# Gate and up of the second layer as one product of 26 block products, with weight sums made in the first layer

## The chip, the cores and the metric

The kernel runs on one core of a Trainium2 chip. The metric is the device time of one execution in microseconds. Three runs of the kernel before took 867.36, 867.67 and 868.07 us; the median is 867.67. The engines are called by these names: TensorE (PE in the profile, PEld for its weight loads), VectorE (DVE), ScalarE (ACT), GpSimd (POOL) and SyncE (SP, which issues the DMAs).

## The reference

Two feed-forward layers follow each other on x of 4 x 512 tokens and 512 features, in float32, each with a residual sum and layer norms without weights:

```
x = x + layernorm(layer1(layernorm(x)))
x = x + layernorm(layer2(layernorm(x)))

layer1(x): s = silu(x @ Wg.T)              # 2048 x 1376
           s = s with the half of each row that is smallest in |s| set to 0
           return (s * (x @ Wu.T)) @ Wd.T
layer2(x): return (silu(x @ Vg.T) * (x @ Vu.T)) @ Vd.T
```

All six weights have 1376 x 512 elements. They come to the kernel transposed, with the contracted dimension first.

## The kernel before

**First layer.** 2048 tokens are 16 tiles of 128, taken two at a time as eight units (`Unit`). For a unit, `products` makes the gate plainly (L433, four contraction chunks, columns in three pieces) and the up product by a seven-product scheme (class `Seven`, L133: 2x2 by 2x2 blocks from 7 block products in place of 8, with sums of the operands made ahead and sums of the products made behind). `search` finds the row threshold by six counts on ScalarE (L485) with small VectorE steps between. `turns` transposes the product, and `finish` makes the down product, again by seven products (`downs`, L234), whose weights are read piece by piece from DRAM (`down_right`, L220, three buffers). These stages of different units overlap: during the gate of unit j the lists `gate` and `up` in `layers` place the down product of unit j-3, the transposes of unit j-2 and the search of unit j-1.

Sums of weights that the seven-product schemes need are made once on VectorE, in `presum` (L180): it loads four blocks of 128 x 1280, makes four sums and stores them to DRAM. Key "a" (down of layer 1) is made in unit 0; "f" (down of layer 2), "g" and "u" (gate and up of layer 2) in unit 1.

**Second layer.** The tokens are four blocks of 512 (`Block`). `norm` normalises and transposes four tiles into xT. `sums` makes four sums of xT on VectorE (`moving_sums`, L125; tile T). Then five groups follow. Group a stands for two pieces of 128 rows of the gate and the two of the same numbers of the up (rows a*128 and 640 + a*128). `pair` (L682) makes both with `Seven`: 7 products each, with two contraction halves in each, so 28 products of 128 x 128 by 256 columns. A product keeps its bank until VectorE has added it to the output (L154 to L168). The product of `silu(gate)` and up is made by L698 and L702, and `down_sums` (L721) makes sums of it on GpSimd (L119 to L122). The last 96 rows of gate and up go through `rest` (L704), one more `Seven`. `finish` (L737) makes the down product and `out_norm` (L344) normalises it, adds the residual and stores.

PSUM has eight banks here: tags pa, px and py with two each for products, and pt with two for transposes.

**What sets the order.** Each engine works off its own instructions in a fixed order. A scheduler at build time chooses that order from a model of the times, with the program's order as priority. `tc.issue_after(i)` puts what is issued inside it behind instruction i on its engine. After the groups of a block the norms of the next block are issued behind `block.mark` (the group's last multiplication), then the next block's `sums`, then this block's `finish`. In block 0 the `finish` of the last unit of layer 1 stands between `sums` and the first group.

The code ends with a second, general path for rows with ties, under a test at run time; it is not taken in these runs.

Of the kernel before, what the change touches and what calls it, by code (L numbers as in the profile page):

```python
# [29 lines left out]

@with_exitstack
def sandwich_kernel(
# [10 lines left out]
):  # L43

# [20 lines left out]
    HC = FULL // 2  # L65
    HF = HC * P
# [26 lines left out]
    presums = {k: dram.tile([4, P, HC * H2], F32, name=f"sum_{k}") for k in ("a", "f", "g", "u")}  # L93
# [86 lines left out]
    def presum(work, key, w_d):  # L180


        down = key in "af"
        bufs = dict(wd=3, hT=2)

        def load(r, c, tag, k):
            t = work.tile([P, HC * H2], F32, tag=tag, name=f"ps_{key}_{k}", bufs=bufs[tag])
            if down:
                src = w_d[r * HF : (r + 1) * HF, c * H2 : (c + 1) * H2]
            else:  # L190
                src = w_d[c * 2 * P : (c + 1) * 2 * P, r * HF : (r + 1) * HF]
            n = HC if down else 2
            nc.sync.dma_start(
                t.rearrange("p (k h) -> p k h", k=n), src.rearrange("(k p) h -> p k h", p=P)
            )
            return t

        def keep(k, t):
            nc.sync.dma_start(presums[key][k - 1], t)

        x = load(0, 1, "wd", "x") if down else load(1, 0, "wd", "x")
        y = load(0, 0, "wd", "y") if down else load(1, 1, "wd", "y")
        z = load(1, 1, "hT", "z") if down else load(0, 0, "hT", "z")
        w = load(1, 0, "wd", "w") if down else load(0, 1, "wd", "w")
        if down:
            nc.vector.tensor_sub(y, x, y)
        else:
            nc.vector.tensor_add(y, x, y)
        keep(1, y)
        nc.vector.tensor_sub(x, z, x)  # L210
        keep(3, x)
        if down:
            nc.vector.tensor_sub(z, z, y)
        else:
            nc.vector.tensor_sub(z, y, z)
        keep(2, z)
        nc.vector.tensor_sub(w, w, z)
        keep(4, w)

# [157 lines left out]
    class Unit:  # L377
# [205 lines left out]
        def turns(self, other=False):  # L583
# [4 lines left out]
            def turn(k, g0):  # L588
                nm = f"{self.nm}_{self.tiles[k]}"
                if g0 == 0:  # L590
                    if other:
                        if k == 0:
                            self.ends = self.work.tile(
                                [P, 2, P], F32, tag="S", name=f"he{nm}", bufs=1
                            )
                        t = self.big.tile([P, 2 * HC, P], F32, tag="b5", name=f"hT{nm}")
                        end = self.ends[:, k, :]
                    else:
                        t = self.work.tile([P, NI, P], F32, tag="hT", name=f"hT{nm}")
                        end = t[:, NI - 1, :]  # L600
                    self.hT.append((t, end[: isz[-1], :]))
                h, (hT, end) = self.p[k], self.hT[k]
                n = min(4, NI - g0)
                pt = psum.tile([P, 4, P], F32, tag="pt", name=f"ph{nm}_{g0}")
                for c in range(n):
                    i = g0 + c
                    nc.tensor.transpose(
                        pt[: isz[i], c, :], h[:, i * P : i * P + isz[i]], ident
                    )
                nf = n if g0 + n <= FULL else n - 1  # L610
                copy = nc.vector.tensor_copy if other and k else nc.scalar.copy
                copy(hT[:, g0 : g0 + nf, :], pt[:, :nf, :])
                if nf < n:
                    copy(end, pt[: isz[-1], nf, :])
# [39 lines left out]
    class Block:  # L654
# [15 lines left out]
        def sums(self):  # L670
            t = [
                self.big.tile([P, 2, 2, N2], F32, tag="b5", name=f"T{self.nm}_{self.b}_{q}")
                for q in range(2)
            ]
            self.right = moving_sums(
                nc.vector,
                *[half[:, :, cols] for half in self.xT for cols in (slice(N2), slice(N2, N))],
                t[0][:, 0], t[0][:, 1], t[1][:, 0], t[1][:, 1],
            )
            self.h = []  # L680

        def pair(self, a, lefts):  # L682
# [6 lines left out]
            sg = self.work.tile([P, 4, N2], F32, tag="w", name=f"sg{nm}", bufs=1)  # L689
            ms = []  # L690
            for k, left, c in zip("gu", lefts, (sg, h)):
                left = {p: w[:, :, ts(a, P)] for p, w in left.items()}
                m = Seven(f"{k}b{nm}", left, self.right, c[:, 1, :], c[:, 2, :], c[:, 3, :])
                m.first()
                ms.append(m)
            c11g, c11u = [m.second() for m in ms]
            nc.scalar.activation(sg[:, 0, :], c11g, AF.Silu)  # L697
            nc.vector.tensor_mul(h[:, 0, :], sg[:, 0, :], c11u)  # L698
            ms[0].third()
            nc.scalar.activation(sg[:, 1:, :], sg[:, 1:, :], AF.Silu)  # L700
            ms[1].third()
            self.mark = nc.vector.tensor_mul(h[:, 1:, :], sg[:, 1:, :], h[:, 1:, :]).ins  # L702

        def rest(self, left):  # L704

            n = I - 2 * HF
            nm = f"{self.nm}_{self.b}"
            t = self.work.tile([P, 4, N2], F32, tag="w", name=f"sgr{nm}", bufs=1)[:n]
            m = Seven(f"rb{nm}", left, self.right, t[:, 0, :], t[:, 1, :], t[:, 2, :])
            m.first()  # L710
            c11 = m.second()
            h = self.big.tile([P, N], F32, tag="b5", name=f"hTb{nm}_r")
            lo, hi = h[:n, :N2], h[:n, N2:]
            nc.scalar.activation(lo, c11, AF.Silu)
            m.third()
            nc.scalar.activation(hi, m.c12, AF.Silu)
            nc.vector.tensor_mul(lo, lo, m.c21)
            nc.vector.tensor_mul(hi, hi, m.c22)
            self.h.append(h)
# [17 lines left out]
        def finish(self, which, wr, final=False):  # L737

            pairs = []
            for q in which:  # L740
                last = lambda i, q=q: self.h[-1][: isz[-1], ts(q + 2 * i, P)]
# [23 lines left out]
    def layers(nm, general):  # L765
        with ExitStack() as sctx:
# [4 lines left out]
            def extra(k, layer):  # L771
                return [
                    wpool.tile([P, 2, 2 * Q], F32, tag=f"w{k}s{q}", name=f"w{k}s{q}{layer}{nm}")
                    for q in range(3)
                ]

# [23 lines left out]
            t1, t2, t4 = extra("u", 1)  # L800
# [23 lines left out]
            else:  # L824
                wr = last_rows(a_wd, 1)
                w_ds = dict(a=a_wd, f=f_wd, g=f_wg, u=f_wu)
                sums_at = {0: "a", 1: "fgu"}
                for j in range(NU):
# [22 lines left out]
                    for k in sums_at.get(j, ""):  # L851
                        presum(work, k, w_ds[k])
                steps = finish(units[-3:-1], wr)
# [14 lines left out]
            lefts, ws = [], []  # L868
            for k, w_d in (("g", f_wg), ("u", f_wu)):
                w = wpool.tile([P, NH, I], F32, tag="w" + k, name=f"w{k}2{nm}")  # L870
                s1, s2, s4 = [y[:, :, :HF] for y in extra(k, 2)]
                a11, a12, a21, a22 = [
                    w[:, 2 * c : 2 * c + 2, r * HF : (r + 1) * HF] for r in range(2) for c in range(2)
                ]
                for q, a in ((1, s1), (2, s2), (3, a21), (4, s4)):
                    nc.sync.dma_start(a, presums[k][q - 1].rearrange("p (k h) -> p k h", k=2))
                for a, c, r in ((a11, 0, 0), (a12, 1, 0), (a22, 1, 1)):
                    nc.sync.dma_start(
                        a,
                        w_d[c * 2 * P : (c + 1) * 2 * P, r * HF : (r + 1) * HF].rearrange(  # L880
                            "(k p) h -> p k h", p=P
                        ),
                    )
                nc.sync.dma_start(
                    w[:, :, 2 * HF :], w_d[:, 2 * HF :].rearrange("(k p) h -> p k h", p=P)
                )
                lefts.append(dict(p1=a11, p2=a12, p3=s4, p4=a22, p5=s1, p6=s2, p7=a21))
                ws.append(w)
            blocks[0].sums()
            if not general:  # L890
                for f in units[-1].turns():
                    f()
                units[-1].down_sums()
                for f in finish([units[-1]], wr):
                    f()
            wr = last_rows(f_wd, 2)
            t = work.tile([P, 3, 2, I - 2 * HF], F32, tag="S", name=f"wrs{nm}", bufs=1)
            rest = stationary_sums(
                nc.vector,
                *[w[:, 2 * c : 2 * c + 2, 2 * HF :] for w in ws for c in range(2)],  # L900
                t[:, 0], t[:, 1], t[:, 2],
            )
            for b, block in enumerate(blocks):
                last = b + 1 == len(blocks)
                for a in range(HC):
                    block.pair(a, lefts)
# [3 lines left out]
                block.rest(rest)  # L910
# [53 lines left out]
```

## Time and profile before

| | |
|---|---|
| median of three runs | 867.67 us |
| the profiled execution | 867.17 us |
| its span, first to last instruction | 865.4 us |
| TensorE busy | 854.2 us, 3642 matmul records |
| VectorE busy | 533.7 us |
| ScalarE busy | 302.5 us |
| GpSimd busy | 98.8 us |
| DMA | 112.96 MB moved |
| first layer | to about 430 us |
| blocks of the second layer start at | 553.2 (1), 655.2 (2), 757.6 us (3) |

The profile is of one execution. In a group's row stand the line, the engine, the operation, out<-in tiles with shapes, the count, then busy us and mean ns of one, then the engine's idle time before and what ended it. A row of a timeline has start, length, engine, line, operation and tiles. Matmuls are pipelined, so the mean of one is its passage and not the spacing of a stream. Matmuls in float32 leave two records each.

### The profile page before, as it was taken

What the parts mean: (1) busy time and instruction counts of PE and PEld (TensorE: products, weight loads), DVE (VectorE), ACT (ScalarE), POOL (GpSimd) and SP (SyncE); (2) the same over time, 40 slices, a digit from 0 to 9 for tenths busy, and PEclk for the clock granted to TensorE, in tenths of its full rate; (3) what the DMA queues carried; (4) which work ended last, traced back from release to release, by engine and by line L of the source; (5) the groups of instructions that cost most, each with busy time, mean ns of one, the idle gap of its engine ahead of it and who ended that gap; (6) DMA issues with size and microseconds to landing.
All of it is one profiled execution on the core that took longest, in us unless ns stands there. A gap on an engine that the chain in (4) does not pass through costs nothing.

```text
span 865.4 us, 10342 instructions
## 1 busy us (share of the span) xinstructions
PE 854.2 (99%) x3642; PEld 659.6 (76%) x3642; DVE 533.7 (62%) x1432; ACT 302.5 (35%) x601; POOL 98.8 (11%) x178
## 2 busy tenths in 40 slices
PE   9999999999999999999999999999999999999996
PEld 5556566767667676677888888888888888888885
DVE  5887787776949677667955445544436445454434
ACT  3465575647474755656111111011111112011100
POOL 1000000000000001000001220121301222012111
PEclk9999999999999999999999999999999999999999
DMA  9999414334233333387573005500054001430032
GB/s 334 372 329 347 177 55 123 122 100 163 67 116 108 123 122 104 100 323 262 169 242 119 0 1 170 189 2 0 18 183 159 1 0 46 153 125 1 0 100 100
DMA packets 60381, 112.96 MB, mean 131 GB/s; under 512 B 4705, under 2 KB 34529, under 8 KB 60321
## 3 DMA queue, kind: packets, MB, share of 16 engines
q1 hardware_dynamic: 60176, 111.95, 38.4%
q8 instruction: 31, 0.51, 0.2%
q14 instruction: 30, 0.24, 0.1%
q10 hardware_dynamic: 144, 0.26, 0.1%
HBM read 93.32 MB, written 18.87 MB: 130 GB/s over the span
## 4 chain that ended last, share of the span: by engine, by line
PE 51%; DVE 2%; ACT 1%; DMA 1%; issue 0%; POOL 0%; ACTq 0%; DVEq 0%
PE pxub L144 6%; PE pxgb L144 6%; PE pxdb L260 6%; PE paub L144 4%; PE pagb L144 4%; PE pydb L260 4%; PE pyub L144 4%; PE pygb L144 4%; PE padb L260 3%; PE pxd L260 2%; PE pyd L260 2%; PE pxrb L144 1%; PE pad L260 1%; ACT ja L485 1%; PE parb L144 1%; PE ptb L373 1%
## 5 line engine op out<-in xcount | busy, mean ns | idle before, releaser
L485 ACT ACTIVATE ja<-v,cur 128x1376 bf16<-128x1376 f32 x96 | 138.4, 1441 | 64.1 <-DVE cur L510 43.0
L433 PE MATMUL pg<-wg,xT 128*128 128x456 f32 (+1 forms) x384 | 154.8, 549 | 0.2 <-ACT p L437 0.2
L433 PEld LDWEIGHTS pg<-wg,xT 128*128 128x128 f32 x384 | 71.9, 190 | 62.7 <-issue 57.6
L144 PE MATMUL pau<-wu,xT 128*128 128x344 f32 x128 | 43.1, 453 | 0.0
L144 PE MATMUL paub<-xTb,wu 128*128 128x256 f32 x160 | 41.3, 380 | 0.1
L144 PE MATMUL pagb<-xTb,wg 128*128 128x256 f32 x160 | 41.1, 379 | 0.0
L144 PE MATMUL pxub<-T,wu 128*128 128x256 f32 x160 | 41.1, 379 | 0.0
L144 PE MATMUL pxgb<-T,wg 128*128 128x256 f32 x160 | 41.1, 379 | 0.0
L260 PE MATMUL pad<-wd_p,hT 128*128 128x256 f32 x160 | 38.9, 380 | 0.1
L437 ACT ACTIVATE p<-pg 128x456 f32<-128x456 f32 (+1 forms) x48 | 26.0, 543 | 36.4 <-PE pg L433 33.1
L260 PE MATMUL pydb<-wdb_p,D 128*128 128x256 f32 x160 | 37.3, 379 | 0.0
L490 DVE TENSOR_SCALAR low<-cur 128x2 int32<-128x2 f32 x48 | 7.9, 165 | 47.1 <-ACT ja L485 46.7
L260 PE MATMUL pxd<-wd_p,hT 128*128 128x256 f32 x160 | 36.8, 379 | 0.0
L119 POOL TENSOR_TENSOR D<-hTb 128x256 f32<-128x256 f32 x20 | 14.6, 729 | 193.9 <-DVE hTb L702 193.9
L260 PE MATMUL padb<-wdb_p,hTb 128*128 128x256 f32 x160 | 36.7, 379 | 0.0
L260 PE MATMUL pxdb<-wdb_p,hTb 128*128 128x256 f32 x160 | 36.2, 379 | 0.0
L260 PEld LDWEIGHTS pad<-wd_p,hT 128*128 128x128 f32 x160 | 29.9, 190 | 6.7 <-DMA wd_p<-in_L_attn_w_down_dram 0.5
L260 PEld LDWEIGHTS pxd<-wd_p,hT 128*128 128x128 f32 x160 | 30.4, 190 | 5.5 <-issue 0.4
L700 ACT ACTIVATE sg<-sg 128x768 f32<-128x768 f32 x20 | 16.9, 843 | 50.3 <-DVE sg L168 50.3
L110 POOL TENSOR_TENSOR rs_o<-ve_o,nhalf 128x1 f32<-128x1 f32 x16 | 11.5, 731 | 198.0 <-DVE ve_o L108 198.0
L144 PEld LDWEIGHTS paub<-xTb,wu 128*128 128x128 f32 x160 | 30.3, 190 | 4.5 <-ACT sg L697 0.4
L260 PEld LDWEIGHTS pxdb<-wdb_p,hTb 128*128 128x128 f32 x160 | 30.4, 190 | 4.2
(245 smaller groups left out, 1699.5 us busy)
## 6 DMA issues: line engine op xcount, KB each, us to landing
wd_p<-sum_a SPq DMA_DIRECT2D x28, 640.0 KB, 4.0
wd_p<-in_L_attn_w_down_dram SPq DMA_DIRECT2D x21, 640.0 KB, 3.9
wdb_p<-sum_f SPq DMA_DIRECT2D x16, 640.0 KB, 4.0
wdb_p<-in_L_ffn_W_down_dram SPq DMA_DIRECT2D x12, 640.0 KB, 3.9
xn<-in_x_dram SPq DMA_DIRECT2D x16, 256.0 KB, 4.1
xr<-in_x_dram SPq DMA_DIRECT2D x16, 256.0 KB, 4.1
x<-y SPq DMA_DIRECT2D x16, 256.0 KB, 3.1
xnb<-x SPq DMA_DIRECT2D x16, 256.0 KB, 4.1
```

What stands on the lines that cost most here:

```text
L110: nc.gpsimd.tensor_tensor(rs, ve, nhalf, ALU.pow)
L119: eng.tensor_add(s1, a21, a22)
L144: nc.tensor.matmul(ps, self.left[k][:, c, :], self.right[k][:, c, :], start=first and c == 0, stop=c == 1, skip_group_check=not first,)
L260: nc.tensor.matmul(p[which], p[1](k, c), ws[k][:, c, :], start=first and c == 0, stop=c == HC - 1, skip_group_check=not first,)
L373: nc.tensor.transpose(pt[:, c, :], xn[:, ts(c, P)], ident)
L433: nc.tensor.matmul(pg, self.xT[:, i, c, :], wg[:, c, c0:c1], start=(c == 0), stop=(c == NH - 1),)
L437: nc.scalar.activation(p[:, c0:c1], pg, AF.Silu)
L485: nc.scalar.activation(junk, v, AF.Sign, bias=cur[:, 0, i : i + 1], accum_out=cur[:, 1, i : i + 1],)
L490: nc.vector.tensor_scalar(low, cur[:, 1, :], 0.0, None, ALU.is_gt)
L700: nc.scalar.activation(sg[:, 1:, :], sg[:, 1:, :], AF.Silu)
```

## The change

**One product for gate and up.** `group` takes the place of `pair`. Tokens (two halves of 256) by contraction (four chunks of 128) is a 2x4 matrix of blocks, contraction by output rows (two of gate, two of up) a 4x4 one. Their product, 32 block products done plainly and 28 before, is made from 26. A line of `PRODUCTS` is one matmul: the bank it goes to (0 to 5), the operand from xT or its sums, the weight operand, and which outputs get the bank's content added or subtracted after it (outputs 0 to 3 for the first half of the tokens, 4 to 7 for the second; by remainder of 4: gate, gate, up, up). Products go on accumulating in a bank, so after an addition the next product into the same bank waits until it has been read, and a bank is read several times.

```diff
+PRODUCTS = (
+    (0, 10, 17, "+2"), (1, 13, 23, "+6"), (2, 14, 24, "+1"), (0, 25, 21, "+6"), (1, 24, 8, "+2"),
+    (3, 3, 12, "+1"), (0, 11, 22, "+4"), (2, 23, 11, "-4-7"), (1, 8, 0, "+0"), (4, 7, 7, "+7"),
+    (3, 20, 13, "+3"), (5, 16, 3, "-7"), (1, 12, 6, "+4"), (0, 15, 2, "+0"), (4, 21, 5, "+5"),
+    (3, 1, 1, "+0"), (1, 4, 9, "+5"), (5, 22, 4, "+0+1"), (0, 2, 25, "+3"), (2, 19, 16, ""),
+    (1, 17, 20, "+1"), (4, 5, 15, "+4"), (0, 9, 14, "+7"), (2, 7, 19, "-6"), (5, 18, 10, ""),
+    (5, 3, 18, "+2"),
+)
```

(In the file each product has a line of its own.)

```diff
-        def pair(self, a, lefts):
+        def group(self, a, w):
...
+            kw = dict(tag="w", bufs=1) if a % 2 == 0 else dict(tag="c")
+            sg = self.work.tile([P, 4, N2], F32, name=f"sg{nm}", **kw)
+            banks, begun = {}, set()
+            left = {m: sum(o % 4 == m for p in PRODUCTS for o in form(p[3])) for m in range(4)}
+            for k, xv, wv, adds in PRODUCTS:
+                first = k not in banks
+                if first:
+                    tag = ("pa", "px", "py")[len(banks) % 3]
+                    banks[k] = bank(tag, f"{tag}b{nm}_{k}")[:, :N2]
+                with ExitStack() as order:
+                    if self.product is not None:
+                        order.enter_context(tc.issue_after(self.product))
+                    self.product = nc.tensor.matmul(
+                        banks[k], w[wv], self.left[xv], start=first, stop=True,
+                        skip_group_check=not first,
+                    ).ins
+                fresh = False
+                for o, s in form(adds).items():
+                    q, m = divmod(o, 4)
+                    c = (sg, h)[m // 2][:, m % 2 * 2 + q, :]
+                    if o in begun:
+                        add = nc.vector.tensor_add if s > 0 else nc.vector.tensor_sub
+                        self.mark = add(c, c, banks[k]).ins
+                    elif fresh:
+                        nc.vector.tensor_scalar(c, banks[k], float(s), None, ALU.mult)
+                    else:
+                        nc.scalar.mul(c, banks[k], float(s))
+                        fresh = True
+                    begun.add(o)
+                    left[m] -= 1
+                    f = m % 2
+                    part = slice(2 * f, 2 * f + 2)
+                    if m == f and not left[f]:
+                        nc.scalar.activation(sg[:, part], sg[:, part], AF.Silu)
+                    if not left[f] and not left[2 + f]:
+                        nc.vector.tensor_mul(h[:, part], sg[:, part], h[:, part])
```

An output's first value is written by ScalarE, later ones are added by VectorE; the mark is the last such add.

**Sums of the tokens.** `Block.sums` makes 18 sums of 128 x 256 on VectorE (`LEFT_SUMS`) in place of four of 128 x 512. In block 0 they are issued behind the last unit's `down_sums`.

**Sums of the weights.** `presum` keeps "a" and "f". For gate and up `weight_sums` is called at the end of units 0 to 4, for groups 4 down to 0: four loads of 256 KB into a tile `area` of 26 operands (16 blocks of weights, ten places more), 17 sums in place (`RIGHT_SUMS`, 15 of two operands at once and two of one), and, except for group 0, a store of the tile to DRAM.

```diff
+        def after_last(part):
+            last = next(
+                i for i in reversed(nc.cur_bb.bb.instructions)
+                if i.engine == mybir.EngineType.DVE
+            )
+            with tc.issue_after(last):
+                for t in part:
+                    step(t)
+        n = 4
+        parts = [RIGHT_SUMS[q : q + n] for q in range(0, len(RIGHT_SUMS), n)]
...
-                sums_at = {0: "a", 1: "fgu"}
+                sums_at = {0: "a", 1: "f"}
+                area = wpool.tile([P, NP, P], F32, tag="ws", name="area")
...
+                    g = NG + 0 - 1 - j
+                    if 0 <= g < NG:
+                        for f in weight_sums(area, g):
+                            f()
```

Group 0 stays in `area`; the 104 operands of groups 1 to 4 are loaded into the tiles that held the first layer's weights.

**The last 96 rows.** `rest` makes gate and up plainly, four contraction chunks of 512 columns each, with SiLU on ScalarE and one multiplication on VectorE; the four weight sums for it go. In block 0 it stands ahead of the last unit's down product.

```diff
-            blocks[0].sums()
-            if not general:
+            if general:
+                blocks[0].sums()
+            else:
                 for f in units[-1].turns():
                     f()
                 units[-1].down_sums()
+                last = nc.cur_bb.bb.instructions[-1]
+                assert last.engine == mybir.EngineType.DVE
+                with tc.issue_after(last):
+                    blocks[0].sums()
+                blocks[0].rest(w_rest)
                 for f in finish([units[-1]], wr):
                     f()
```

Smaller moves: the ends of the hidden tiles of the last units but one get a tag of their own ("he"), and the scratch of a group alternates between the tags "w" and "c".

## The prediction

> **What bounds the kernel now.** I read the page's head first, then the stretches of time, the groups by shape, the chain of waits and the timeline at a change of block.
>
> ```profile
> PE 854.2 (99%) x3642; PEld 659.6 (76%) x3642; DVE 533.7 (62%) x1432; ACT 302.5 (35%) x601; POOL 98.8 (11%) x178
> ```
>
> TensorE is busy for 99% of the span. That matmuls overlap could hide gaps, so the spacing decides, not this share. The chain of waits names few others and gives the spacing:
>
> ```profile
> PE 51%; DVE 2%; ACT 1%; DMA 1%; issue 0%; POOL 0%; ACTq 0%; DVEq 0%
> ```
>
> ```profile
> 639.84 4.32 PE padb L260 x20
> 644.16 0.86 PE padb L266 x4
> ```
>
> 20 records take 4.32 us: 0.216 us each. In fp32 every product of 128x128 by 256 columns leaves two records (the second layer's groups show 20 x 28 x 2 = 1120), so a product costs 0.432 us. Stretches of the first and second layer (PE, PEld, DVE, ACT, POOL, clock, DMA):
>
> ```profile
> 50.00:100.00 50.00, 50.00 (x148) 27.52 (x147) 43.52 (x106) 24.99 (x52) 1.42 (x4) 1.00 0.83 304
> 200.00:250.00 50.00, 50.00 (x193) 33.48 (x192) 37.51 (x118) 30.57 (x57) 2.68 (x6) 1.00 0.39 124
> 655.00:757.00 102.00, 102.00 (x482) 88.66 (x481) 50.83 (x120) 14.98 (x35) 18.89 (x28) 1.00 0.21 68
> ```
>
> TensorE has no gap in any of them, at full clock. VectorE works 75% of a first-layer stretch and half of a block. So a product taken away is worth its 0.432 us, as long as VectorE follows.
>
> The Trainium skill, "Perfetto Trace Analysis", section "Identifying the Most-Contended Engine", says matmul busy time misjudges headroom and weight loads should be read: by that, 88.66 of 102 leaves 13% free on TensorE and the saving could vanish into slack. The spacing above says otherwise: 0.19 us of load in every 0.216 us slot is 88% with no slot empty. The measurement decides; by the rule the sum would be near zero.
>
> **TensorE, the certain part.** A group of one block drops from 28 products (7 of two contraction halves, gate and up) to 26. 20 groups x 2 x 0.432 = 17.3 us saved. The 96 left-over rows go from 14 products, 6.05 us, to 8 plain ones of 512 columns. The nearest wide row is 16 records of 456 columns in 6.28 us; less the last one's overhang of 0.165 that is 0.382 each, the same 0.84 ns a column as 256 columns show. So 512 columns give 0.43 a record, 0.86 a product, 6.9 a block: 4 x 0.83 = 3.4 us lost. Net -13.9 us.
>
> **VectorE in a group, and the waits of the banks.**
>
> ```profile
> L154 DVE TENSOR_TENSOR sg<-sg,pxgb 128x256 f32<-128x256 f32 x20 | 8.4, 420 | 7.0 <-ACT sg L153 6.6 <-PE pxgb L144 0.4
> L153 ACT COPY sg<-pagb 128x256 f32<-128x256 f32 x20 | 7.4, 372 | 67.5 <-PE pagb L144 34.5 <-DVE hTb L702 32.9
> L127 DVE TENSOR_TENSOR T<-xTb 128x512 f32<-128x512 f32 x4 | 2.8, 688 | 2.9 <-ACT xTb L375 2.9
> ```
>
> The table of products asks for 26 updates of outputs: 8 first ones, which go to ScalarE at 0.37, and 18 adds on VectorE at 0.42, beside two multiplications of 512 elements at 0.69. VectorE gets 18 x 0.42 + 2 x 0.69 = 8.9 us in 26 x 0.432 = 11.2, against 11 x 0.42 + 0.96 = 5.6 in 12.1 now. It fits, but it is no longer slack. ScalarE has 8 x 0.37 + 2 x 0.6 = 4.2 (its rows show 0.54 for 456 and 0.84 for 768 elements).
>
> Now a bank is written again before the group ends, so products wait for reads. In the timeline at 553.17 two products run, their end is due at 554.03 and the copy starts at 554.23: 0.20 after the last slot. A product begun at t is thus read from t+0.63 and free at t+1.00 (ScalarE) or t+1.05 (VectorE). At 437.48 a ScalarE read ends and the weight load that waited starts at 437.53: 0.05. The load runs 0.216 ahead of its product. A bank is reused three products later at the soonest, load at t+1.08, against 1.05 and 1.10: one reuse by VectorE per group is 0.02 late. VectorE's queue (two adds for one product, then the next) makes another up to 0.1 late. 20 groups x 0.02 to 0.12 = 0.4 to 2.4 us; I take 1.
>
> **Starts of blocks.** Here in-order VectorE is still at the normalisation of the block before:
>
> ```profile
> 655.00 0.85 DVE L329 TENSOR_TENSOR yb<-yb,pydb 128x256 f32<-128x256 f32 x2 [0.53 <-PE pydb L266]
> 655.76 1.28 DVE L104 BATCH_NORM_STATS2 st_ob<-yb 128x6 f32<-128x512 f32 x2
> 656.96 0.30 DVE L106 BATCH_NORM_AGGREGATE mv_ob<-st_ob 128x2 f32<-128x6 f32 x2
> 657.22 0.42 DVE L154 TENSOR_TENSOR sg<-sg,pxgb 128x256 f32<-128x256 f32 x1
> ...
> 658.63 1.42 DVE L359 SCALAR_TENSOR_TENSOR yb<-yb,rs_ob,xrb 128x512 f32<-128x512 f32 x2
> 659.96 0.41 DVE L154 TENSOR_TENSOR hTb<-hTb,pxub 128x256 f32<-128x256 f32 x1
> ```
>
> The block starts at 655.23, VectorE is free at 660. One add slipped in at 657.22, the other stood behind both L359 and cost nothing, since its bank was not needed. In the new order the add of product 4 (numbered from 0) is ready at 655.23 + 4 x 0.432 + 0.63 = 657.59 and its bank is due for product 8 at 658.69. Placed where the second L154 stands it ends at 660.38; product 8 starts at 660.64, 1.95 late. Slipped in at 658.5 it costs 0.5, then product 10 another 0.6. If product 3's add stands behind L359 too, product 6, due at 657.82, is 2.8 late; if the order puts adds first, nothing is lost. So 0 to 2.8 a block, and 1.5 from the trace's own mix; three blocks: 4.5 (0 to 8.4).
>
> The sums over the tokens grow from 4 x 0.69 to 18 x 0.42 = 7.6 us on VectorE. Before blocks 1 to 3 they lie beside 34 us of down products, where VectorE has more than half free: nothing. Before block 0 they are pinned after the last unit's transposed sums, which end at 440.25, so they end near 448. Today seven products of group 0 at 0.86, 6.05 us, fill the holes of 433.86 to 450.93; afterwards the 6.9 us of left-over rows must. Its weights land last of the loads. I take +1 (-1 to 4).
>
> **First layer.** Gone: 8 subtractions at 1.49 and 4 at 0.35, 13.3 us. New: per unit 0 to 4, 15 sums of 256 elements at 0.42 and 2 of 128 at about 0.3 (the 192-element row shows 0.35): 6.9, in all 34.5. A 50 us stretch leaves VectorE 12.5 idle, and the second unit carried 12 x 1.49 = 17.9 of such sums (50 to 100 in the view above) with TensorE full. That cover hides it; without it a search chain would be up to 6.9 a unit later, against one unit of slack. On SyncE's queue: 8 loads and 8 stores of 640 KB leave, 20 loads of 256 KB and 4 stores of 1664 KB come, now also in units 2 to 4, where the 640 KB loads of down weights land in 4 us and are wanted soon after. A store in front could delay one by up to 4 us in three units: 0 to 12, nearest to the loads that already share the queue at no price. I take 1. The second layer's loads shrink from 14 x 640 KB to 104 x 64 KB, at the same place.
>
> **Sum.** -13.9 + 1 + 4.5 + 1 + 1 = -6.4. The profiled execution took 867.17 (span 865.4 and 1.8 around it), which gives 860.8; the median shown lies 0.5 above it, so 861.3.
>
> The skill's "VectorE: DVE Perf Modes", section "Rules for kernel authors", speaks against the change: keep the number of operations on VectorE small, since each waits for the pipeline to empty. By its reading every add would stand alone, which the 0.42 us above already charges; it changes the sum only where adds queue.
>
> **Rivals.** First, a clean cover: adds come first in VectorE's order, stores disturb nothing. -13.9 + 0.5 gives 853.8 profiled, 854.3. For it: 8.9 of 11.2 us fits. Against it: the trace's L359 ahead of the add. Chance 0.25.
>
> Second, VectorE's backlog drags: 2.8 at each of four block starts, 2.4 in groups and no net cover in the first layer, about 12 lost: 866 to 869, no measurable change. For it: VectorE goes from 46% to 80% inside groups and cannot catch up in one. Chance 0.12.
>
> Third, slower: the hand-over of a bank takes longer than I read. It sits at three reuses per group at distance three. The group saves 0.86 and the left-over rows take back 0.17, so it decides when each of the three is 0.23 us late, a hand-over of 1.3 instead of 1.05. At 1.45, 20 x 3 x 0.37 = 22 us are lost and with the 4.5 of block starts it ends near 882 (-13.9 + 22 + 4.5 + 2). Against it: the 0.05 us release at 437.53. Chance 0.15.
>
> That the change does not do what it says would mean TensorE's records do not fall by 80 in the groups; the tables leave no room for that.
>
> **How the numbers follow.** Forecast (faster, 856 to 865.9) 0.48, clean 0.25, backlog 0.12, slow hand-over 0.15. A run of this kernel tells about 0.2%, 1.7 us, from no change. Faster 0.73, same 0.12, slower 0.15. The range takes in clean and backlog with the bounds of 0.4 in groups: 853.5 to 869.5.
>
> **What would show it.** Group products: 1040 records at 0.216, left-over rows 64 at 0.43. Right: a block's period falls from 102.3 to near 100.6 (5 x 0.864 less 0.83 saved, 1.5 and 0.25 waited), and weight loads wait for VectorE's adds for some 1.5 us at each block's start and hardly inside groups. Wrong: TensorE idle in the first layer after a late down weight; waits spread over all groups; a hole above 2 us between 430 and 460.

## The result, and the profile after

The changed kernel takes **859.30 us** (median of five runs, 858.18 to 860.42), the kernel before 867.36 in the five runs beside them. The ratio is 0.9908, 95% interval 0.9894 to 0.9923: 8.1 us faster. The profiled execution took 859.3 with a span of 857.4, against 865.4 before: 8.0 less.

The head of the page after:

```profile
PE 842.7 (98%) x3514; PEld 635.5 (74%) x3514; DVE 615.2 (72%) x1697; ACT 345.5 (40%) x713; POOL 100.7 (12%) x178
```

TensorE has 128 records fewer: 80 in the groups and 48 in the left-over rows (14 products of two records became eight, per block). VectorE has 81 us more work, and TensorE's share falls from 99 to 98%: the holes have grown. The chain of waits can't show them, because it breaks off at the last instructions:

```profile
DVE 0%; issue 0%; POOLq 0%
```

So the timeline has to be read. Stretches of time (length, then busy us of PE, PEld, DVE, ACT, POOL, clock, DMA share, GB/s):

```profile
50.00:100.00 50.00, 50.00 (x149) 27.70 (x148) 41.55 (x124) 30.40 (x56) 1.76 (x4) 1.00 0.55 198
200.00:250.00 50.00, 50.00 (x195) 33.93 (x194) 41.77 (x130) 29.72 (x56) 3.83 (x4) 1.00 0.45 138
430.00:462.00 32.00, 30.43 (x130) 21.56 (x128) 20.27 (x50) 6.15 (x16) 1.82 (x3) 1.00 0.67 222
553.00:655.00 102.00, 101.33 (x460) 84.14 (x458) 68.58 (x177) 26.33 (x66) 19.70 (x30) 1.00 0.26 84
```

The first layer is as full as it was. In the changeover (430 to 462) 1.57 us of TensorE are free by this view, against 0.51 before. In a block of the second layer VectorE goes from half to two thirds and TensorE loses 0.67. The rows of the new work:

```profile
L824 DVE TENSOR_TENSOR sg<-sg,pxb 128x256 f32<-128x256 f32 x80 | 33.7, 421 | 18.9 <-PE pxb L814 16.5 <-PE pyb L814 0.4
L828 ACT ACTIVATE hTb<-pab 128x256 f32<-128x256 f32 x40 | 15.4, 384 | 57.6 <-PE pab L814 52.4 <-PE pxd L374 5.2
L846 PE MATMUL parb<-xTb,w_rest 128*96 128x512 f32 x32 | 14.6, 594 | 0.0
```

VectorE's adds take 421 ns each and ScalarE's first writes 384, and over the run both wait mostly for TensorE; TensorE waits for them only in the places listed below.

**Where the time went.** I counted TensorE's late time: from each start, subtract the starts before it plus their records at their spacing (0.216 us for 256 columns, 0.43 for 512). The 17.3 less 3.4 of the prediction's certain part is 13.9; what came back is this:

| place | us late beyond before |
|---|---|
| first layer (last transposes ahead of the changeover at 429.40, before 429.92) | -0.5 |
| changeover, 430 to 460 (2.95, before 1.33) | +1.6 |
| first group of block 0 | +0.4 |
| a down weight of block 0 lands late, 536.26 (1.3, before 0.3) | +1.0 |
| starts of blocks 1, 2, 3 | +1.2, +0.6, +1.1 |
| down products of block 3, between 829.14 and 835.92 | +0.3 |
| inside the other groups | 0 |

-13.9 - 0.5 + 6.2 = -8.2, and the span says -8.0. The four kinds of hole, seen on TensorE. In the changeover:

```profile
442.49 0.70 PE L374 MATMUL pz<-wr,hT 96*128 96x256 f32 x2 [0.75 <-ACT hT L722]
...
449.45 2.43 PE L368 MATMUL pad<-wd_p,hT 128*128 128x256 f32 x10 [0.28 <-DMA wd_p<-in_L_attn_w_down_dram]
...
452.14 2.32 PE L368 MATMUL pxd<-wd_p,hT 128*128 128x256 f32 x10
454.98 2.42 PE L368 MATMUL pxd<-wd_p,hT 128*128 128x256 f32 x10 [0.51 <-DVE y L396]
...
529.87 4.48 PE L368 MATMUL pxdb<-wdb_p,hTb 128*128 128x256 f32 x20
534.18 0.60 PE L481 MATMUL ptb<-ident,xnb 128*128 128x128 f32 x4
...
536.26 4.58 PE L368 MATMUL padb<-wdb_p,hTb 128*128 128x256 f32 x20 [1.05 <-DMA wdb_p<-in_L_ffn_W_down_dram]
```

Two products into the same bank `pxd` now follow each other directly, so the second waits until VectorE's L396 has read the first. Before, two products of group 0 stood between them (450.07 and 450.93); in the order that the scheduler chose for the changed kernel nothing does. VectorE is not busy with the token sums at that moment: it ended the last of them at 451.10 and stood idle for the 1.77 us before L396.

```profile
450.68 0.42 DVE L277 TENSOR_TENSOR Ts<-xTb,T 128x256 f32<-128x256 f32 x1
...
454.50 0.42 DVE L396 TENSOR_TENSOR y<-y,pxd 128x256 f32<-128x256 f32 x1 [1.77 <-PE pxd L368]
```

20 records still take 4.31 us (529.87 to 534.18), 0.216 each, so the spacing is unchanged.

The start of block 1, at 552.35, on VectorE and then on TensorE:

```profile
552.12 0.85 DVE L437 TENSOR_TENSOR yb<-yb,pydb 128x256 f32<-128x256 f32 x2 [0.53 <-PE pydb L374]
552.89 1.28 DVE L170 BATCH_NORM_STATS2 st_ob<-yb 128x6 f32<-128x512 f32 x2
...
554.35 0.42 DVE L824 TENSOR_TENSOR hTb<-hTb,pab 128x256 f32<-128x256 f32 x1
...
555.60 0.41 DVE L824 TENSOR_TENSOR hTb<-hTb,pxb 128x256 f32<-128x256 f32 x1
555.93 0.42 DVE L824 TENSOR_TENSOR sg<-sg,pab 128x256 f32<-128x256 f32 x1
...
557.49 0.75 DVE L467 SCALAR_TENSOR_TENSOR yb<-yb,rs_ob,xrb 128x512 f32<-128x512 f32 x1 [0.48 <-DMA xrb<-x]
...
559.02 0.42 DVE L824 TENSOR_TENSOR hTb<-hTb,pxb 128x256 f32<-128x256 f32 x1
```

```profile
555.37 0.59 PE L814 MATMUL pyb<-Ts,area 128*128 128x256 f32 x2
556.07 0.70 PE L814 MATMUL pxb<-T,area 128*128 128x256 f32 x2
...
558.33 0.59 PE L814 MATMUL pab<-T,area 128*128 128x256 f32 x2
559.50 0.70 PE L814 MATMUL pxb<-T,area 128*128 128x256 f32 x2 [0.57 <-DVE hTb L824]
560.03 0.59 PE L814 MATMUL pab<-xTb,area 128*128 128x256 f32 x2
```

Three adds slip in between the parts of the normalisation, so product 8 (556.07, due at 555.80) is only 0.27 late. The second L467 then waits 0.48 for the residual's load with the adds queued behind it; the add at 559.02 ends at 559.44 and product 14 starts at 559.50, 0.74 after its slot. With 0.1 for the slower start after each wait that makes 1.2. The residual's load is a small part of it: block 3 has the same order without that wait and is 0.58 late at product 14.

### The profile page after: what moved, and what is told of

Read it like the earlier page. It is cut to its first block, busy times and chain, and to the rows that moved or that the text cites. A ratio compares the mean times of both kernels' runs of the same rounds, so it can differ in the third digit from the quotient of the medians.

```text
span 857.4 us, 10620 instructions
## 1 busy us (share of the span) xinstructions
PE 842.7 (98%) x3514; PEld 635.5 (74%) x3514; DVE 615.2 (72%) x1697; ACT 345.5 (40%) x713; POOL 100.7 (12%) x178
## 5 line engine op out<-in xcount | busy, mean ns | idle before, releaser
L824 DVE TENSOR_TENSOR sg<-sg,pxb 128x256 f32<-128x256 f32 x80 | 33.7, 421 | 18.9 <-PE pxb L814 16.5
L835 ACT ACTIVATE sg<-sg 128x512 f32<-128x512 f32 x40 | 23.0, 622 | 47.9 <-DVE sg L824 47.9
L828 ACT ACTIVATE hTb<-pab 128x256 f32<-128x256 f32 x40 | 15.4, 384 | 57.6 <-PE pab L814 52.4
L720 ACT COPY hT<-ph 128x512 f32<-128x512 f32 (+1 forms) x45 | 22.7, 511 | 29.5 <-PE ph L715 23.9
L368 PEld LDWEIGHTS padb<-wdb_p,hTb 128*128 128x128 f32 x160 | 30.3, 190 | 5.6 <-DMA wdb_p<-in_L_ffn_W_down_dram 1.4
L210 PEld LDWEIGHTS pau<-wu,xT 128*128 128x128 f32 x128 | 23.8, 190 | 13.6 <-issue 4.3
L368 PEld LDWEIGHTS pydb<-wdb_p,D 128*128 128x128 f32 x160 | 30.2, 190 | 4.1
```

The source lines that it names most:

```text
L210: nc.tensor.matmul(ps, self.left[k][:, c, :], self.right[k][:, c, :], start=first and c == 0, stop=c == 1, skip_group_check=not first,)
L368: nc.tensor.matmul(p[which], p[1](k, c), ws[k][:, c, :], start=first and c == 0, stop=c == HC - 1, skip_group_check=not first,)
L824: self.mark = add(c, c, banks[k]).ins
L828: nc.scalar.mul(c, banks[k], float(s))
L835: nc.scalar.activation(sg[:, part], sg[:, part], AF.Silu)
```

## The experiments

The theory after the result: TensorE's work fell as computed, banks and first layer cost nothing, and the rest sits where VectorE's in-order queue holds something back: the token sums of block 0 and the normalisations at the block starts. The rivals: a slow hand-over of banks; the weight sums in the first layer; the order of the left-over rows. Each kernel was timed in five rounds (e4 and e10 in three) beside the kernel before, and each ratio is to that kernel. The kernel before had medians of 867.36 beside the changed kernel, 866.78 beside e1 to e4, 867.07 beside e5 to e8 and 867.75 beside e9 and e10, so a difference between kernels of different sets is uncertain by up to 1 us.

**The left-over rows alone**, on the kernel before:

```diff
-            m = Seven(f"rb{nm}", left, self.right, t[:, 0, :], t[:, 1, :], t[:, 2, :])
...
+            ps = [bank(k, f"{k}rb{nm}")[:n, :] for k in ("pa", "px")]
+            for c, t in zip(ps, w):
+                for k in range(NH):
+                    nc.tensor.matmul(
+                        c, t[:, k, :], self.xT[k // 2][:, k % 2, :],
+                        start=k == 0, stop=k == NH - 1,
+                    )
...
-            rest = stationary_sums(
...
+            rest = [w[:, :, 2 * HF :] for w in ws]
```

> The kernel before with one part of the change alone: the last 96 rows of gate and up made plainly, 8 products of 512 columns a block in place of 14 of 256. By the prediction's sum TensorE gives up 4 x 0.83 = 3.4 us and nothing else moves: about 870.8 us against 867.4, ratio 1.004. A rival says that the lighter work on VectorE (one multiplication for seven operations, no weight sums) pays it back: 867 to 868, ratio 1.000 to 1.001; then the 26 products alone would be worth less than 17.3.

871.14 against 866.78, ratio 1.0050 [1.0032, 1.0068]: 4.3 us slower, 2.8 to 5.9 by the interval. The 3.4 of the prediction lies inside. The profiled run is 2.8 us longer than the profiled run of the kernel before (868.2 against 865.4): by the count records make 3.45 more, the first layer loses 1.3 less, what follows it 0.3 more, and the end behind the last matmul is 0.4 longer. So the size is that of the prediction, and the lighter VectorE pays none of it back.

**Weight sums left out:**

```diff
                 for t in part:
-                    step(t)
+                    pass
...
+                nc.gpsimd.memset(area[:, 16:, :], 0.5)
```

> The changed kernel without the arithmetic of the weight sums in the first layer (85 VectorE operations, 34 us, left out; a constant stands in their places, so the second layer multiplies by other numbers); loads and stores stay. If VectorE's idle time hides them, as predicted, the time stays at 859.3, within 1 us. If they delay the search or the change between the layers, it falls by 2 to 6 us.

858.79, ratio 0.9907 [0.9891, 0.9923], as the changed kernel. 34 us of VectorE's work are hidden in the first layer, as the stretches above say.

**All first writes on VectorE**, to see when VectorE does become the bound:

```diff
-                    elif fresh:
-                        nc.vector.tensor_scalar(c, banks[k], float(s), None, ALU.mult)
                     else:
-                        nc.scalar.mul(c, banks[k], float(s))
-                        fresh = True
+                        nc.vector.tensor_scalar(c, banks[k], float(s), None, ALU.mult)
```

> The changed kernel with the 8 first writes of a group moved from ScalarE to VectorE: 26 operations of about 0.42 and two of 0.69, 12.3 us of VectorE for 11.2 us of products. If an operation holds VectorE for its whole 0.42 us, VectorE becomes the bound of the groups: 20 x 1.1 = 22 us more, about 881. If operations that do not depend on each other follow at 0.34, 26 x 0.36 + 1.3 = 10.7 us fit under the products and only the tight reuses wait: 861 to 866.

869.90, ratio 1.0035 [1.0025, 1.0044]: 10.6 above the changed kernel, between the two numbers. A group grows from 11.22 to 11.65 us, by 0.32 of waiting and 0.1 of a slower start at one bank, and the block starts wait longer. TensorE's weight loads, what they waited for (us in total, times, longest):

```profile
PEld pxb L814 <- DVE hTb L826: 10.2, 18, 0.6
PEld pxb L814 <- DVE hTb L824: 4.4, 8, 1.0
```

18 waits for the same write: one place of the table, product 4's bank, in nearly every group. That a group with 12.3 us of busy VectorE takes 11.65 shows that busy time overlaps too (below). Without ScalarE's share of the writes the change would have cost 3.1 us instead of gaining 8.1.

**Banks reused two products later** instead of three, by exchanging products 2 and 3:

```diff
-    (2, 14, 24, "+1"),
     (0, 25, 21, "+6"),
+    (2, 14, 24, "+1"),
```

> The changed kernel with products 2 and 3 of a group exchanged, so that a bank is written again two products after its first in place of three. By the hand-over that the prediction read (free 1.05 us after the product's start, weight load 0.22 ahead) the load due at t+0.65 waits until t+1.05: 0.40 us in each of 20 groups, 8 us, about 867. If the weights are loaded before the wait, only 0.19 is lost, 3.7 us: 863. If the hand-over is already slower than read, more than 0.5 each: 870 or more.

865.23, ratio 0.9963 [0.9950, 0.9976]: 5.9 above the changed kernel by the medians, 7.0 by the spans. The waits of the weight loads, and a start of a group on TensorE and ScalarE:

```profile
PEld pab L814 <- ACT hTb L828: 8.8, 18, 0.5
```

```profile
589.99 0.59 PE L814 MATMUL pab<-T,wu 128*128 128x256 f32 x2
590.43 0.59 PE L814 MATMUL pxb<-T,wu 128*128 128x256 f32 x2
591.12 0.70 PE L814 MATMUL pab<-Ts,wu 128*128 128x256 f32 x2
```

```profile
590.69 0.38 ACT L828 ACTIVATE hTb<-pab 128x256 f32<-128x256 f32 x1 [1.04 <-PE pab L814]
```

The read starts 0.70 after the product and ends 1.08 after it; the product two places on starts at 1.13 instead of 0.86, 0.27 late, and another 0.1 goes with the slower start: 0.37 in a group. The four later groups of block 0 lose 0.32 each and its first nothing; from 430 us on the count gives 6.1 more late time in all, and 0.8 of the 7.0 lies in the first 50 us. By the two ratios the difference is 4.8. The hand-over is 1.08, the slow one (1.3 or more) falls, and three products, 1.30, cover it.

**The last normalisations later in the program's order:**

```diff
-                    out_norm(work, tiles[0], ya, res, dst, nm)
+                    late.append(lambda ...: out_norm(...))   # in the last piece of downs
...
                     block.group(a, w_of[a * NP : (a + 1) * NP])
+                    while late:
+                        late.pop(0)()
```

> The changed kernel with the last two normalisations of each block's output put behind the first group of the next block in program order, so that VectorE adds the first products before it normalises. The trace of the changed kernel shows TensorE waits of 1.2, 0.6 and 1.1 us in the first group of blocks 1 to 3. By the theory of the in-order queue these go: 859.3 - 2.9 = 856.4, ratio to the kernel before 0.9875. If the hand-over of the banks itself is slow, waits stay where they are and the time is 859.3; if the normalisations then collide with later groups, they come back there, 859 or more.

858.56, ratio 0.9900 [0.9883, 0.9918]. At the starts of blocks 1 and 3 VectorE's order stayed the same, since the scheduler chooses among what its model takes to be ready, and 1.0 us was lost at each (1.2 and 1.1 in the changed kernel). At block 2 the order did change. The first adds moved up among the parts of the two normalisations, and one add stands between the two last parts, which ran one after the other in the changed kernel (655.88):

```profile
656.19 0.75 DVE L469 SCALAR_TENSOR_TENSOR yb<-yb,rs_ob,xrb 128x512 f32<-128x512 f32 x1
656.85 0.42 DVE L826 TENSOR_TENSOR sg<-sg,pyb 128x256 f32<-128x256 f32 x1
657.18 0.75 DVE L469 SCALAR_TENSOR_TENSOR yb<-yb,rs_ob,xrb 128x512 f32<-128x512 f32 x1
```

There the late time fell from 0.6 to 0.2, with both normalisations still in one group. The gain is too small for the time of the whole kernel to show it. To move the normalisations in all blocks they were **tied down**, behind product 5's add of the next block's first group:

```diff
+                        if ip == 5:
+                            self.early = self.mark
...
+                    with tc.issue_after(block.early):
+                        while late:
+                            late.pop(0)()
```

> As e3_late_norms, but with the VectorE work of the two last normalisations of a block tied behind the third add of the next block's first group (the one for product 5), since a place later in the program did not change VectorE's order. If the waits at block starts come from VectorE standing in the normalisation, they fall from 2.9 us in three blocks to under 0.6: about 856.9, ratio to the kernel before 0.988. If normalisation and adds simply do not fit together in one group, the waits move some products further and the time stays at 859.

859.90, ratio 0.9919 [0.9905, 0.9932]: nothing gained. The waits moved within the group and are the same in all three blocks. TensorE at block 1:

```profile
559.31 0.70 PE L816 MATMUL pxb<-xTb,area 128*128 128x256 f32 x2
560.64 0.70 PE L816 MATMUL pyb<-T,area 128*128 128x256 f32 x2 [0.63 <-DVE hTb L826]
```

Product 8 is on time now and product 17 is 0.9 late, with 0.27 before it at product 14: some 1.4 a block with the slower starts, where the changed kernel has 1.2, 0.6 and 1.1. A normalisation is 2.24 us of VectorE (0.69 + 0.17 + 0.15 + 0.48 + 0.75 in the timeline), and by the prediction's 8.9 a group leaves 11.2 - 8.9 = 2.3: one fits into a group and two don't. But that sum counts every operation at its full length, which overstates VectorE (last section), and block 2 of e3 has two in one group with 0.2 lost. There they begin at 652.50, 0.5 after the block, and fill the time until the first products can be read; in e5 VectorE first stands idle for 1.38 (before 554.00) and begins them at 555.20. So two leave little room in a group, and what they cost depends on when they begin and where the adds stand among their parts.

**The token sums made twice:**

```diff
-                signed_add(nc.vector, t, v[a], sa, v[b], sb)
+                for _ in range(2):
+                    signed_add(nc.vector, t, v[a], sa, v[b], sb)
```

> The changed kernel with each of the 18 token sums made twice in place (7 us more VectorE per block, same values). By the prediction the sums of blocks 1 to 3 lie under the down products and cost nothing, those of block 0 stand in VectorE's queue before the first sum of the last unit's down product and cost up to 7 us: 862 to 866. If all blocks paid, 880 or more; if none does, 859.3.

863.41, ratio 0.9953 [0.9940, 0.9967]: 4.1 more. The waits of TensorE that grew:

```profile
PE padb L368 <- DMA wdb_p<-in_L_ffn_W_down_dram: 2.5, 1, 2.5
PE pxd L368 <- DVE y L396: 2.2, 1, 2.2
```

The second is in the changeover: VectorE works without a pause from 442.33 to 458.56, and L396 has its turn only at 456.47. By the count that changeover costs 1.9 more. The first is the late down weight of block 0, and it costs more than the wait:

```profile
538.86 2.08 PE L368 MATMUL padb<-wdb_p,hTb 128*128 128x256 f32 x4 [2.54 <-DMA wdb_p<-in_L_ffn_W_down_dram]
```

After it the granted clock of TensorE was 0.51 from 538.8 to 542.0 (1.00 before and after), and its records start some 0.43 apart in place of 0.216, which costs 1.6 us in all. After the wait of 2.1 in e8 below the clock stayed at 1.00. This profiled execution is the slowest of its five (864.42), so the others may have less of it. The starts of blocks 2 and 3 did not change; that of block 1 grew from 1.2 to 1.9, behind the late weight and beside its own doubled sums, which the run doesn't separate. So the sums are free before blocks 2 and 3 and not free before block 0.

**Block 0's token sums earlier**, ahead of the last unit's transposes and not tied:

```diff
+                blocks[0].sums()
                 for f in units[-1].turns():
                     f()
                 units[-1].down_sums()
-                last = nc.cur_bb.bb.instructions[-1]
-                assert last.engine == mybir.EngineType.DVE
-                with tc.issue_after(last):
-                    blocks[0].sums()
```

> The changed kernel with the token sums of block 0 not tied behind the last unit's transposed sums but ahead of its transposes, where VectorE stands idle for 2.6 and 3.5 us (434.8 to 442.3 in the trace). By the theory that these sums hold up the last unit's down product, its wait of 0.7 us (454.98) goes and group 0 can fill more: 858 to 858.6. If the early sums stand in front of the transposed sums instead, the hole at 442 grows and the time is 860 or more.

857.28, ratio 0.9886 [0.9871, 0.9901]. The holes at 449 and 455 are gone: a piece of the down product into another bank stands between the two of `pxd` (448.96 and 453.71).

```profile
451.12 2.32 PE L368 MATMUL pad<-wd_p,hT 128*128 128x256 f32 x10
```

Group 0 fills no more than in the changed kernel, three products in both, so it is the order of the pieces that helped. What is left is the wait for ScalarE's last transposed piece at 443.

**Block 0's left-over rows after its groups** (`blocks[0].rest(w_rest)` removed ahead of the down product):

```diff
-                blocks[0].rest(w_rest)
...
-                if b or general:
-                    block.rest(w_rest)
+                block.rest(w_rest)
```

> The changed kernel with the 96 left-over rows of block 0 after its groups, as in the other blocks. By the prediction they are the 6.9 us that fill TensorE's holes between 430 and 450 in place of group 0: without them TensorE stands idle there, and the time grows by 3 to 7 us, to 862 to 866. If other work fills the holes, 859.3.

859.25, ratio 0.9907 [0.9892, 0.9923]: no change, but other holes:

```profile
PE pad L368 <- DMA wd_p<-in_L_attn_w_down_dram: 2.1, 1, 2.1
PE pz L374 <- ACT hT L722: 0.8, 1, 0.8
```

The hole at 442 stays as it was (0.8, now at 435.75), so the rows did not fill it: they ran at 430.5 to 437.9 in the changed kernel, before the holes. Without them the down product starts earlier and waits 2.1 for its own weights instead of 0.3, so what the rows did cover is that load; the late down weight at 536 is gone.

**Both cures:** early token sums, and the two last normalisations tied into two groups, one in each:

```diff
+                    if late:
+                        with tc.issue_after(block.early):
+                            late.pop(0)()
```

> e7_early_token_sums, and of the two last normalisations of a block one tied behind the third add of the next block's group 0 and the other behind that of group 1. A group leaves VectorE some 2.2 us, a normalisation takes 2.2, and two in one group were too much in e5 (waits of 1.3 us a block). If that is the reason, the waits at the starts of blocks 1 to 3 fall from 2.9 in all to under 1: 857.3 - 2 = 855.3, ratio to the kernel before 0.986. If each normalisation costs its wait wherever it lies, 857.3.

**855.43**, ratio 0.9850 [0.9827, 0.9873], the fastest of all. The waits of its TensorE of 0.5 us and more, behind the very first:

```profile
PE ph L717 <- DVE hT L722: 0.8, 1, 0.8
PE pz L374 <- ACT hT L724: 0.8, 1, 0.8
PE pxdb L368 <- DMA wdb_p<-sum_f: 0.6, 1, 0.6
PE padb L368 <- DMA wdb_p<-in_L_ffn_W_down_dram: 0.5, 1, 0.5
```

No product of a group is among them; by the count one starts 0.23 late, in block 1. The starts of the three blocks lose 0.3 in all, against 2.7 in e7. From 430 us on 3.7 us of late time went against the changed kernel, and the span fell by 3.5 (857.4 to 853.9).

## Why the prediction was right, and where its sizes were not

The forecast of 861.3 was the right case: sign and main mechanism hold. It has 6.4 us gained where 8.1 were, 1.7 too little; the other 0.3 between 861.3 and 859.3 is the kernel before, 867.36 here and 867.67 there. By its steps:

- **TensorE, the certain part (-13.9): right.** 1040 records in the groups, and 64 for the left-over rows, four of them in 1.72 us (432.26 to 433.98). Alone the rows cost 4.3 [2.8, 5.9] where 3.4 was said (4 x 0.83 is 3.3). The slack of 13% that the Trainium skill's "Perfetto Trace Analysis", section "Identifying the Most-Contended Engine", would have read from the weight loads was not there: in the steady groups the whole saving came through, 11.22 us for 12.1.
- **VectorE in a group (+1): mis-sized, it is 0.** A group takes 11.22 us, 26 x 0.432 being 11.23. The hand-over was read rightly: in steady state (changed kernel),

```profile
564.78 0.59 PE L814 MATMUL pab<-T,wg 128*128 128x256 f32 x2
...
565.47 0.38 ACT L828 ACTIVATE hTb<-pab 128x256 f32<-128x256 f32 x1 [1.04 <-PE pab L814]
...
565.91 0.36 PEld L814 LDWEIGHTS pab<-Ts,wg 128*128 128x128 f32 x2
...
566.08 0.59 PE L814 MATMUL pab<-Ts,wg 128*128 128x256 f32 x2
```

  the read starts at 0.69 (0.63 was said), ends at 1.07, the load follows at 1.13, and the product is still on time at 1.30: a load 0.17 ahead is early enough, where 0.216 was assumed. The queue of adds was charged too dearly, 0.42 each (last section).
- **Starts of blocks (+4.5): mis-sized, 2.9.** The mechanism is the one named, adds among the last normalisation. The order came out better than the trace's mix: three adds slip in, product 8 loses 0.27, and product 14, which the prediction did not name, loses more. What decides is when the normalisations begin and where the adds stand among their parts: two in one group, both behind the third add, cost 1.4 a block (e5), two begun at once with the first adds among their parts 0.2 (e3, block 2), and one in each of two groups almost nothing (e9).
- **Block 0's start (+1): mis-sized, 2.0** (1.6 and 0.4). "Afterwards the 6.9 us of left-over rows must" fill the holes was wrong: they run before them, and e8 takes them away without making the hole at 442 longer. The sums ended at 451.10, not near 448. What opened are two pieces of the down product into `pxd` directly behind each other (0.8), a wait of the piece into `pad` for its weights (0.6, of the kind that cost 0.3 before) and some 0.6 more at the transposes and what waits for them (430.47 and 442.49). The order on TensorE is what e7 changes, and it loses 1.4 less; only with twice the sums (e6) does VectorE's queue itself hold the read of `pxd` back, by 1.7 more. Why the scheduler chose that order is not shown.
- **First layer (+1): mis-sized, -0.5.** Cover there is, for sums (e2) and transfers alike; no late down weight appears in it.
- **Missing from the sum: +1.0 at 536.26,** a late down weight in the second layer. Its load is issued beside another of 640 KB and the loads of the tokens, and the two loads of this kind between 520 and 540 us landed in 6.4 (median, 4.0 in the kernel before), where all twelve of the page have 3.9. e6 lengthens the wait and e8 removes it, but e2 and e5, which change nothing there, lose only 0.35 and 0.6, so a part of it differs from one execution to the next. That the loads collide is read from the trace and not shown by a run: a further weight buffer was not tried.

Against the forecast, 1.0 less in groups, 1.6 less at the block starts and 1.5 less in the first layer, with 1.0 more in the changeover and 1.3 more for the late down weight and block 3's wait, make -1.8, which is the 1.7. A block's period, which was to fall to 100.6, is 99.6 and 99.3 (starts at 552.35, 651.98 and 751.29).

Of the rivals, the clean cover (854.3) was the nearest miss: it is what e9 gives at 855.43. The backlog is what e4 makes by giving VectorE the eight writes too: waits in nearly every group and 869.9, about its price (866 to 869; its terms add up to 13.6 and not to 12, which that range holds). The slow hand-over is excluded by e10.

## What to carry to other kernels

When the bound engine loses work, look at the few places where an in-order engine behind it has other work due, not at its mean share: here 0 us were lost in the steady groups, 2.9 at the starts of blocks and 2.0 between the layers. Work that has to go into a stream with slack should go in small parts between the operations that are due: begun late and all in one period it only moves the wait (e5), spread over two periods it costs almost nothing (e9). And the effect of an edit of the program's order has to be looked up place by place in the trace: e3 changed the engine's order at one block start and not at the other two.

## What the runs showed of the hardware

VectorE's adds are 0.42 us long but follow each other every 0.33 to 0.34 us when none needs the result of the one before. Six token sums in the changeover:

```profile
446.66 2.10 DVE L277 TENSOR_TENSOR T<-xTb,T 128x256 f32<-128x256 f32 x6
...
454.96 0.42 DVE L403 TENSOR_TENSOR y<-y,pyd 128x256 f32<-128x256 f32 x1
455.41 0.42 DVE L404 TENSOR_TENSOR y<-y,pz 128x256 f32<-128x256 f32 x1
```

(2.10 - 0.42) / 5 is 0.336, while L404, which needs L403's output, follows after 0.45. So up to a fifth of a sum of busy times is overlap, and 12.3 us of it went through 11.65 in e4. The Trainium skill, "VectorE: DVE Perf Modes", section "The DRAIN you can't avoid", says that the next operation doesn't start until the pipe is empty, and adds that one which is not held starts earlier; the rows agree with the addition.

After each wait counted above TensorE lost 0.1 us more than the wait: the product behind it takes 0.53 (559.50 to 560.03 at the start of block 1) instead of 0.432.
